# Tap windows kept as a ring of padded rows, in a fused channel-attention and involution kernel

## The chip, the cores and the metric

The kernel runs on one core of a Trainium2 chip. The metric is the device time in microseconds (us) of one launch, the median of the timed runs; the profile is one more execution of the same program. Engines are named as in the profile: PE is TensorE, DVE is VectorE, ACT is ScalarE, POOL is GpSimd, SP is SyncE, which issues most of the transfers.

## What is computed

The input is x of shape (4, 512, 64, 64), float32. Layer 0 is attention over the 4096 pixels of each image; layer 1 is an involution block: a 7x7 stencil whose weights differ from pixel to pixel and are shared by groups of 16 channels.

```python
# layer 0, n = 64*64 pixels
q, k, v = wq@x + bq, wk@x + bk, wv@x + bv          # 128 channels each
attn = softmax(q^T k)                              # 4096 x 4096
x = wo @ (v attn^T) + bo + x
# layer 1, 8 groups of 16 channels, K = 7
o = relu(s1 * (W1 @ x) + b1)                       # 128 channels
w = Ws @ relu(sr * (Wr @ o) + br) + bs             # 49 taps * 8 groups per pixel
y[c, h, w] = sum over taps (i, j): w[g(c), i, j, h, w] * pad(o)[c, h + i, w + j]
out = s3 * (W3 @ y) + b3 + x
```

## The kernel before

`fast_path` does everything; `general_path` is a fallback that a final test on the softmax sums (rls, verdict) selects, and it does not run on these inputs. The outer loop goes over the 4 images (batches, b).

**Attention.** `keys_values(b)` makes k and v for 8 chunks of 512 pixels (tiles xa). `attention(b)` then takes 8 blocks of 512 query pixels (tiles xb; in the last batch the last block is two halves of 256). For each block it goes over 32 key tiles of 128: a score matmul (pss, 128x512), an exponential on ACT (pt, five buffers), a value matmul accumulated in po, and a running sum of pt on DVE (pacc, line 522). TensorE is fed with this steady stream, and everything else is slipped in between: after each step the kernel calls `chores()`.

**Three queues of chores.** They are Python generators; each `yield` ends a step, and the order in which the steps are called is the order of the instructions on each engine.
- `finishing` (`finish_block`): normalises a block of attention (pl, rl), projects it (pwo, line 418, and the addition to xb on line 420), computes o (p, line 428), transposes it (pp) and writes it as pixel rows into a padded image in DRAM (pix, lines 454 to 460), and computes the reduced features (red).
- `taps` (`involution`): the stencil, in units of 4 image rows, 16 units (u) per batch. A unit lives as 128 partitions (two image rows of 64 pixels) x NT = 2 row pairs x 128 channels. The weights of all 49 taps come from a pair of matmuls into PSUM (pw, two banks, one buffer, line 218). Each product is one DVE instruction (line 264) over two taps, that is 2 row pairs x 2 taps x 128 channels = 512 elements per partition (the 49th tap gives one of 256); GpSimd adds it to acc (line 285). One more GpSimd addition (line 294) folds the two halves of acc.
- `closing` (`turn_unit`, `close_chunk`): transposes the sum of a unit on TensorE (pa, line 308) and, for every second unit, applies W3 (py, line 324), adds the result to xb on DVE (line 326) and stores the chunk (line 332).

**The windows of pixels.** A product needs, on the partition of each output pixel, the shifted pixels of its row pair. They are loaded from pix by overlapping reads in `pump()`: for each unit two tiles, with 4 and with 3 horizontal shifts (SHIFTS), each of SR = 9 rows; copies of the first kind have two buffers, of the second one. Each is two transfers of 64 partitions. A unit is begun only when all rows of its window are in pix, that is its own 4 rows and 3 of the next unit, or when the image is complete (line 470).

**Pacing.** The kernel keeps its own estimate of engine time while it writes the program: `pe` for TensorE, and `free` for DVE, GpSimd and DMA, from constants on lines 54 to 60. `pace()` lets out at most TAPS_A_US products per us of TensorE time; `involution` holds a product back while its windows are not due to have landed, or while DVE or GpSimd would be more than 3.5 or 7.5 us behind. `turn_unit` issues its transposes 2 us after the sum is due (line 300). [...] When attention of the last batch has been written, `tail` is set: nothing is held back any more, and every second product is summed by TensorE with an identity matmul into PSUM (accp, line 279) rather than by GpSimd, and joined by a DVE addition (line 293).

The x tiles (xa and xb alike) have six buffers. A tile of xb lives until its chunk is stored.

## Time and profile before

| | |
|---|---|
| device time, median of 3 (lowest to highest) | 2767.58 us (2766.44 to 2768.6) |
| span of the profiled execution | 2761.0 us |
| mean granted TensorE clock | 0.987 |
| products on DVE (line 264, prod), count and busy | 1536, 974.0 us |
| sums on GpSimd (line 285), 512 elements, count and busy | 1412, 1798.2 us |
| window transfers (copies from pix), count and size | 128 of 1152 KB, 128 of 864 KB |
| all transfers | 377.78 MB, mean 137 GB/s |

The page of the profile gives totals per engine, then the span in 40 slices of 69 us (each digit is a share in tenths), then groups of instructions with their count, busy time, mean duration and the idle time ahead of them with what ended it. `prod<-copies,pw` means that the instruction writes prod and reads copies and pw. An fp32 matmul is two instructions in the profile, so 6694 of them are some 3350 matmuls of the program. Idle time of an engine that does not set the pace costs nothing.

### The profile page before, as it was taken

The page shows a single profiled execution, that of the slowest core. Times are in us where ns is not written, and L with a number is a line of the kernel's source. Part 1 is how long each engine was busy: PE and PEld are TensorE (multiplying, and loading weights), DVE is VectorE, ACT ScalarE, POOL GpSimd, SP SyncE. Part 2 cuts the span into 40 slices and gives each one's busy share as a digit, 9 for nine tenths or more (in the row PEclk, how much of TensorE's full clock was granted, in tenths as well). Part 3 has the DMA queues.
Part 4 walks back from the last instruction along what each step waited for, and adds up shares of the span by engine and source line. Part 5 has one row for each costly group of instructions (what it writes and reads, how often), then busy time and mean ns, then how long its engine had stood idle before and what let it go on. Part 6 is the DMA issues. An engine that isn't in the chain of part 4 may idle for free.

```text
span 2761.0 us, 24223 instructions
## 1 busy us (share of the span) xinstructions
PE 2679.7 (97%) x6694; PEld 1205.4 (44%) x6694; DVE 1951.8 (71%) x3091; ACT 894.5 (32%) x1514; POOL 1892.8 (69%) x1548
## 2 busy tenths in 40 slices
PE   8999999999899999999999999999989999999986
PEld 4444444444344444444444444444434444444742
DVE  0356888786586678777566687788747758787886
ACT  2333333332233333333233333333323333333410
POOL 0004887788785478778876477787877548787875
PEclk9999999999999999999999999999999999999998
DMA  6033566668844567766863367766894445666695
GB/s 238 16 64 71 115 144 146 144 136 219 176 113 95 108 145 154 154 141 139 207 158 81 84 114 151 154 136 147 185 227 120 110 88 119 140 143 130 143 195 124
DMA packets 223057, 377.78 MB, mean 137 GB/s; under 512 B 7928, under 2 KB 100288, under 8 KB 222784
## 3 DMA queue, kind: packets, MB, share of 16 engines
q1 hardware_dynamic: 222624, 374.74, 61.6%
q8 instruction: 54, 0.88, 0.1%
q10 hardware_dynamic: 288, 1.42, 0.1%
q14 instruction: 91, 0.75, 0.1%
HBM read 333.29 MB, written 42.77 MB: 136 GB/s over the span
## 4 chain that ended last, share of the span: by engine, by line
PE 91%; DVE 3%; POOL 3%; DMA 1%; issue 0%; ACT 0%; POOLq 0%; SPq 0%; DVEq 0%; ACTq 0%
PE pss L168 32%; PE po L168 32%; PE p L168 4%; PE pq L168 4%; PE py L168 4%; PE pwo L168 4%; PE pk L168 3%; PE pv L168 3%; POOL acc L285 3%; DVE prod L264 2%; PE pw L168 2%; PE pl L168 1%; PE pr L168 1%; PE accp L168 1%; PE pa L308 1%; DMA copies<-pix 1%
## 5 line engine op out<-in xcount | busy, mean ns | idle before, releaser
L285 POOL TENSOR_TENSOR acc<-acc,prod 128x512 f32<-128x512 f32 x1476 | 1844.9, 1250 | 843.8 <-DVE prod L264 538.0
L168 PE MATMUL pss<-q,k 128*128 128x512 f32 (+1 forms) x2112 | 1055.5, 582 | 0.0
L168 PE MATMUL po<-pt,v 128*128 128x512 f32 (+1 forms) x2112 | 1052.4, 580 | 0.0
L264 DVE TENSOR_TENSOR prod<-copies,pw 128x512 f32<-128x512 f32 (+1 forms) x1536 | 974.0, 670 | 89.2 <-POOL acc L285 79.5
L496 ACT ACTIVATE pt<-pss 128x512 f32<-128x512 f32 (+1 forms) x1056 | 616.5, 584 | 1213.7 <-PE pss L168 1080.0
L522 DVE TENSOR_TENSOR pacc<-pacc,pt 128x512 f32<-128x512 f32 (+1 forms) x990 | 672.5, 679 | 451.5 <-ACT pt L496 443.1
L168 PEld LDWEIGHTS po<-pt,v 128*128 128x128 f32 x2112 | 399.6, 190 | 480.8 <-issue 464.4
L168 PEld LDWEIGHTS pss<-q,k 128*128 128x128 f32 x2112 | 393.6, 190 | 466.4 <-issue 455.0
L168 PE MATMUL pwo<-on,wt 128*128 128x512 f32 (+1 forms) x264 | 131.6, 584 | 5.2 <-DVE xb L420 5.2
L168 PE MATMUL py<-accT,wt 128*128 128x512 f32 (+1 forms) x264 | 134.0, 596 | 2.0 <-ACT accT L311 2.0
L168 PE MATMUL pq<-xb,wt 128*128 128x512 f32 (+1 forms) x264 | 120.4, 600 | 8.2 <-DVE xb L326 8.2
L411 DVE RECIPROCAL rl<-pl 128x128 f32<-128x128 f32 x128 | 118.6, 941 | 12.6 <-PE pl L168 12.6
L168 PE MATMUL p<-xb,wt 128*128 128x512 f32 (+1 forms) x264 | 123.3, 593 | 2.4 <-DVE xb L420 2.4
L437 ACT ACTIVATE xb<-xb,vec 128x512 f32<-128x512 f32 (+1 forms) x132 | 93.0, 707 | 98.8 <-PE p L168 94.4
L168 PE MATMUL pk<-xa,wt 128*128 128x512 f32 x256 | 123.4, 623 | 0.3 <-DMA xa<-x_dram 0.3
L168 PE MATMUL pv<-xa,wt 128*128 128x512 f32 x256 | 116.1, 593 | 0.0
L326 DVE SCALAR_TENSOR_TENSOR xb<-py,vec,xb 128x512 f32<-128x512 f32 (+1 forms) x132 | 96.3, 732 | 20.5 <-PE py L168 20.2
L420 DVE SCALAR_TENSOR_TENSOR xb<-pwo,bo,xb 128x512 f32<-128x512 f32 (+1 forms) x132 | 96.2, 732 | 19.7 <-PE pwo L168 19.2
L264 DVE TENSOR_TENSOR acc<-copies,pw 128x512 f32<-128x512 f32 x64 | 43.4, 678 | 89.0 <-PE pw L168 88.9
L520 DVE COPY pacc<-pt 128x512 f32<-128x512 f32 (+1 forms) x33 | 22.3, 677 | 88.5 <-ACT pt L496 88.5
L168 PEld LDWEIGHTS pq<-xb,wt 128*128 128x128 f32 x264 | 51.4, 197 | 68.2 <-issue 54.0
L168 PEld LDWEIGHTS p<-xb,wt 128*128 128x128 f32 x264 | 51.2, 195 | 64.5 <-issue 55.3
(49 smaller groups left out, 875.0 us busy)
## 6 DMA issues: line engine op xcount, KB each, us to landing
copies<-pix SPq DMA_DIRECT2D x128, 1152.0 KB, 13.4
copies<-pix SPq DMA_DIRECT2D x128, 864.0 KB, 14.3
xa<-x_dram SPq DMA_DIRECT2D x32, 1024.0 KB, 11.8
xb<-x_dram SPq DMA_DIRECT2D x32, 1024.0 KB, 6.0
out_dram<-xb SPq DMA_DIRECT2D x31, 1024.0 KB, 9.6
pix<-o1t SPq DMA_DIRECT2D x62, 128.0 KB, 2.5
wt<-wts_dram ACTq DMA_DIRECT2D x1, 1284.0 KB
out_dram<-xb SPq DMA_DIRECT2D x2, 512.0 KB, 3.5
```

The source lines that it names most:

```text
L168: nc.tensor.matmul(o, lhsT=lhsT, rhs=rhs, start=start, stop=stop)
L264: nc.vector.tensor_tensor(prod[:, :, :n, :].rearrange("p t d (g c) -> p t d g c", g=G), image.rearrange("p t d (g c) -> p t d g c", g=G), ...
L285: nc.gpsimd.tensor_tensor(acc[:, :, :n, :], acc[:, :, :n, :], prod[:, :, :n, :], ALU.add)
L308: nc.tensor.transpose(pa[:, t, :], acc[:, t, 0, :], ident)
L326: nc.vector.scalar_tensor_tensor(xt[:, t, :], py, v1(V_S3 + t), xt[:, t, :], ALU.mult, ALU.add)
L411: nc.vector.reciprocal(rl[:, cols], pl[:, cols])
L420: nc.vector.scalar_tensor_tensor(xt[:, t, :], pw, bo[:, t : t + 1], xt[:, t, :], ALU.add, ALU.add)
L437: nc.scalar.activation(xt[:, t, :], xt[:, t, :], AF.Identity, bias=v1(V_B3 + t))
L496: nc.scalar.activation(pt, pss, AF.Exp)
L520: nc.vector.tensor_copy(paccs[k], pt)
L522: nc.vector.tensor_tensor(paccs[k], paccs[k], pt, ALU.add)
```

## The change

The windows are kept in one ring of 12 padded rows with all 7 horizontal shifts (`ring`, 12 x 7 x 128 elements per partition). Each row of an image is loaded into the ring once, instead of once for each of the units whose windows contain it; `low` is the first row still needed and `load` the next to be loaded, and rows go in as their pixels are written and as earlier ones are done with (`pump`). The batches' rows are numbered in steps of 72.

A product now covers 4 or 3 taps that lie above one another (DYS), one horizontal shift at a time, so up to 2 x 4 x 128 = 1024 elements. Where the rows of such a run would cross the end of the ring, it is cut into 2 + 2 or 2 + 1 taps. acc becomes four taps wide and is folded by two GpSimd additions. prods has four buffers of twice the size. `pace` counts taps instead of products. The weights' columns are reordered to match (host side, not shown).

A unit is put into the queue with its own 4 rows; the products with the taps of rows 0 to 3 need no more than these, and those with rows 4 to 6 wait in the generator for the next unit's rows.

In the last batch the last two blocks of attention, instead of the last one, are done in halves of 256 queries, and a step of a half takes two key tiles, so that exponentials and running sums stay 512 wide (the row sums are then added by two matmuls, pl). In the tail the identity matmuls of a unit are joined with its last transposes: the four parts of acc and the two parts of accp, copied to SBUF, are summed by TensorE while they are transposed. Some steps of `finish_block` follow one another faster for the late blocks.

```diff
+WP = W + 2 * PAD
+RING = 12
+STEP = 72
 SR = UR + K - 2
-WP = W + 2 * PAD
-SHIFTS = (0, 4), (4, 3)
-TAPS_A_US = 0.78
+DYS = (0, 4), (4, 3)
+TAPS_A_US = 1.56
 PE_COLUMN = 0.43 / 256
 DVE_OP, POOL_OP = 0.7, 1.28
-COPY_US, X_US, PIX_US, LAND_US = (5.9, 4.4), 3.8, 1.5, 3.0
+DVE_TAPS, POOL_TAPS = (0.16, 0.27), (0.19, 0.55)
+ROW_US, X_US, PIX_US, LAND_US = 2.2, 3.8, 1.5, 3.0
...
-    sapool = pool("sa", 2)
-    sbpool = pool("sb", 1)
     redpool = pool("red", 3)
     work1 = pool("work1", 1)
     work2 = pool("work2", 2)
-    prods = pool("prods", 7)
+    prods = pool("prods", 4)
...
+    ring = const.tile([P, RING, K, P], F32, name="ring")
...
-        due, seen = min(due + TAPS_A_US * (pe - seen), 10), pe
+        due, seen = min(due + TAPS_A_US * (pe - seen), 20), pe
         for _ in range(2):
-            if due < 1 or not step(taps, 1):
+            if due < 2 or not step(taps, 1):
                 break
-            due -= 1
     def pump():
-        for task in list(pending):
-            b, u, part, written = task
-            if not spare[part]:
-                continue
-            pending.remove(task)
-            spare[part] -= 1
-            dx, n = SHIFTS[part]
-            copies = (sapool, sbpool)[part].tile(
-                [P, SR, n, P], F32, tag="s", name=f"copies_{b}_{u}_{part}"
-            )
+        nonlocal load
+        while load // STEP in written:
+            b, row = divmod(load, STEP)
+            rows, us = written[b]
+            end = H + SR - UR if rows == H else rows + PAD - 1
+            n = min(b * STEP + end, low + RING) - load
+            n = min(n, RING - load % RING)
+            if n <= 0:
+                break
             for h in range(2):
-                rows = pix[b % 2][UR * u + h : UR * u + h + SR, dx : dx + W, :]
+                src = pix[b % 2][row + h : row + h + n, :W, :]
                 windows = bass.AP(
-                    tensor=rows.tensor, offset=rows.offset, ap=[[P, W], [WP * P, SR], [1, n * P]]
+                    tensor=src.tensor, offset=src.offset, ap=[[P, W], [WP * P, n], [1, K * P]]
                 )
                 nc.sync.dma_start(
-                    copies[h * W : (h + 1) * W].rearrange("p r x c -> p r (x c)"), windows
-                )
-            free["dma"] = max(free["dma"], written)
-            loaded[b, u, part] = copies, takes("dma", COPY_US[part]) + LAND_US
+                    ring[h * W : (h + 1) * W, load % RING : load % RING + n]
+                    .rearrange("p r x c -> p r (x c)"),
+                    windows,
+                )
+            free["dma"] = max(free["dma"], us)
+            us = takes("dma", ROW_US * n) + LAND_US
+            landing.update((load + i, us) for i in range(n))
+            load += n
+            if row + n == H + SR - UR:
+                load = (b + 1) * STEP
...
-            acc = work2.tile([P, NT, 2, P], F32, tag="acc", name=f"acc_{b}_{u}")
+            acc = work2.tile([P, NT, 4, P], F32, tag="acc", name=f"acc_{b}_{u}")
...
+            accp, ops = None, []
+            base = b * STEP + u * UR
+            for dy0, n in DYS:
+                at = (base + dy0) % RING
+                whole = at + n + NT < RING + 1
+                pieces = [(dy0, n)] if whole else [(dy0, 2), (dy0 + 2, n - 2)]
+                ops += [(x, dy, k) for x in range(K) for dy, k in pieces]
+            for o, (x, dy, n) in enumerate(ops):
+                if o and dy >= DYS[1][0] > ops[o - 1][1]:
+                    low = base + UR
+                    pump()
+                rows = [(base + dy + t * 2) % RING for t in range(NT)]
+                while base + dy + n + NT > load:
+                    yield "wait"
+                landed = max(landing[base + dy + i] for i in range(n + NT))
+                while not tail and (
+                    pe < max(begin, landed)
+                    or free["dve"] > pe + 3.5
+                    or free["pool"] > pe + 7.5
+                ):
+                    yield "wait"
+                free["pool"] = max(free["pool"], takes("dve", DVE_TAPS[0] + DVE_TAPS[1] * n))
+                takes("pool", POOL_TAPS[0] + POOL_TAPS[1] * n)
+                due -= n
+                d0 = dy - DYS[dy >= DYS[1][0]][0]
+                first = x == 0 and dy < DYS[1][0]
+                prod, p0 = acc, d0
+                if not first:
+                    prod, p0 = prods.tile(
+                        [P, NT, 4, P], F32, tag="prod", name=f"prod_{b}_{u}_{o}"
+                    ), 0
+                col = (x * K + dy) * G
+                lines = ring[:, rows[0] : rows[0] + n, x, :]
+                image = bass.AP(
+                    tensor=lines.tensor, offset=lines.offset,
+                    ap=[lines.ap[0], [(rows[1] - rows[0]) * K * P, NT], [K * P, n], [1, P]],
+                )
+                nc.vector.tensor_tensor(
+                    prod[:, :, p0 : p0 + n, :].rearrange("p t d (g c) -> p t d g c", g=G),
+                    image.rearrange("p t d (g c) -> p t d g c", g=G),
+                    pw[:, :, col : col + n * G].unsqueeze(3)
+                    .broadcast_to([P, NT, n * G, GC])
+                    .rearrange("p t (d g) c -> p t d g c", d=n),
+                    ALU.mult,
+                )
+                if first:
+                    pass
+                elif tail and o % 2 and (accp is not None or n > 1):
+                    begin_sum = accp is None
+                    if begin_sum:
+                        accp = ps1.tile(
+                            [P, NT, 2, P], F32, tag=("po", "acc")[u % 2], name=f"accp_{b}_{u}"
                         )
+                    for d in range(0, n, 2):
+                        k = min(2, n - d)
+                        mm(
+                            accp[:, :, :k, :], ident, prod[:, :, d : d + k, :],
+                            begin_sum and d == 0, o + 2 >= len(ops) and d + 2 >= n,
+                        )
+                else:
+                    nc.gpsimd.tensor_tensor(
+                        acc[:, :, d0 : d0 + n, :], acc[:, :, d0 : d0 + n, :], prod[:, :, :n, :],
+                        ALU.add,
                     )
+                yield
+            low = max(low, (b + 1) * STEP if u == NU - 1 else base + UR)
+            pump()
+            if accp is None:
+                for n in (2, 1):
+                    nc.gpsimd.tensor_tensor(
+                        acc[:, :, :n, :], acc[:, :, :n, :], acc[:, :, n : 2 * n, :], ALU.add
+                    )
...
-        for t in range(NT):
-            nc.tensor.transpose(pa[:, t, :], acc[:, t, 0, :], ident)
-        pe_us(0.25)
+        if accp is None:
+            for t in range(NT):
+                nc.tensor.transpose(pa[:, t, :], acc[:, t, 0, :], ident)
+            pe_us(0.25)
+        else:
+            accs = work1.tile([P, CH // P, P], F32, tag="o1t", name=f"accs_{b}_{u}")
+            nc.scalar.copy(accs, accp.rearrange("p t d c -> p (t d) c"))
+            for t in range(NT):
+                parts = [acc[:, t, d, :] for d in range(4)] + [accs[:, 2 * t + d, :] for d in range(2)]
+                for i, part in enumerate(parts):
+                    mm(pa[:, t, :], part, ident, i == 0, i == len(parts) - 1)
...
         rows = top + n // W
-        while begun[b] < NU and (begun[b] * UR + UR + PAD <= rows or rows == H):
-            u = begun[b]
-            begun[b] += 1
-            pending.extend((b, u, part, written) for part in range(2))
-            units.append((b, u))
+        written[b] = rows, us
+        units.extend((b, u) for u in range(top // UR, rows // UR))
         pump()
...
-            blocks[-1:] = [(NCH - 1, off, CH // 2) for off in (0, CH // 2)]
+            blocks[-2:] = [(c, off, CH // 2) for c in (NCH - 2, NCH - 1) for off in (0, CH // 2)]
+        steps = [(k, j) for k, (_, _, n) in enumerate(blocks) for j in range(N // P * n // CH)]
         qs, pts, pos, paccs = {}, {}, {}, {}
         qs[0] = queries(b, *blocks[0])
         def score(m):
-            k, j = divmod(m, nj)
+            k, j = steps[m]
             n = blocks[k][2]
-            pss = ps.tile([P, CH], F32, tag="s", name=f"pss_{b}_{k}_{j}")[:, :n]
-            mm(pss, kt[:, j * P : (j + 1) * P], qs[k])
-            pt = ptpool.tile([P, CH], F32, tag="pt", name=f"pt_{b}_{k}_{j}")[:, :n]
+            pss = ps.tile([P, CH], F32, tag="s", name=f"pss_{b}_{k}_{j}")
+            for i in range(CH // n):
+                key = (j * (CH // n) + i) * P
+                mm(pss[:, i * n : (i + 1) * n], kt[:, key : key + P], qs[k])
+            pt = ptpool.tile([P, CH], F32, tag="pt", name=f"pt_{b}_{k}_{j}")
             nc.scalar.activation(pt, pss, AF.Exp)
             pts[m] = pt
         score(0)
         score(1)
-        for m in range(len(blocks) * nj):
-            k, j = divmod(m, nj)
+        for m, (k, j) in enumerate(steps):
             c, off, n = blocks[k]
+            nj = N // P * n // CH
             if j == 0:
                 pos[k] = ps1.tile([P, CH], F32, tag="po", name=f"po_{b}_{k}")[:, :n]
-                paccs[k] = ps1.tile([P, CH], F32, tag="acc", name=f"pacc_{b}_{k}")[:, :n]
+                paccs[k] = ps1.tile([P, CH], F32, tag="acc", name=f"pacc_{b}_{k}")
...
             pt = pts.pop(m)
-            mm(pos[k], vT[:, j, :], pt, j == 0, j == nj - 1)
-            takes("dve", DVE_OP * n / CH)
+            for i in range(CH // n):
+                key = j * (CH // n) + i
+                mm(
+                    pos[k], vT[:, key, :], pt[:, i * n : (i + 1) * n],
+                    key == 0, key == N // P - 1,
+                )
+            takes("dve", DVE_OP)
             if j == 0:
                 nc.vector.tensor_copy(paccs[k], pt)
             elif j < nj - 1:
                 nc.vector.tensor_tensor(paccs[k], paccs[k], pt, ALU.add)
             else:
-                sums = work1.tile([P, CH], F32, tag="sums", name=f"sums_{b}_{k}")[:, :n]
+                sums = work1.tile([P, CH], F32, tag="sums", name=f"sums_{b}_{k}")
                 nc.vector.tensor_tensor(sums, paccs.pop(k), pt, ALU.add)
```

## The prediction

> **What bounds the kernel now.** I read the page's totals and slices first, then busy time by stage, then the waits inside the odd stages, then single instructions.
>
> ```profile
> PE 2679.7 (97%) x6694; PEld 1205.4 (44%) x6694; DVE 1951.8 (71%) x3091; ACT 894.5 (32%) x1514; POOL 1892.8 (69%) x1548
> PE   8999999999899999999999999999989999999986
> PEclk9999999999999999999999999999999999999998
> DMA  6033566668844567766863367766894445666695
> ```
>
> TensorE is the wall almost everywhere; VectorE and GpSimd have 30% free. The two 8s inside the PE row, near 690 and 2000 us, and its last two digits are where time can be had. How much? The first tap-weight matmul of batches 1 and 2 (the timeline):
>
> ```profile
> 842.50 0.93 PE L168 MATMUL pw<-wt,red 33*128 33x392 f32 x4
> 1508.39 0.93 PE L168 MATMUL pw<-wt,red 33*128 33x392 f32 x4
> ```
>
> One batch takes 665.9 us. Its TensorE work: 8 chunks x 82 matmuls of 512 columns plus 64 for keys and values = 720; consecutive pairs start 1.717 us apart in the timeline, so 0.858 each, 618 us; 16 tap-weight sets at 0.86, 14; 96 transposes at 0.108, 10. Sum 642. So **24 us per batch are lost**, and busy time by stretches of 10 us shows where more than half goes:
>
> ```profile
> 700.00:710.00 10.00, 7.27 (x17) 3.27 (x16) 5.93 (x10) 1.17 (x2) 9.37 (x9) 0.84 1.05 247
> 710.00:720.00 10.00, 3.83 (x12) 1.62 (x11) 5.78 (x9) 0.00 (x0) 9.45 (x9) 0.84 1.05 207
> 720.00:730.00 10.00, 9.27 (x20) 3.75 (x19) 4.13 (x6) 2.16 (x4) 9.37 (x9) 0.81 1.09 255
> ```
>
> Columns: PE, PEld, DVE, ACT, POOL busy, granted clock, DMA share, GB/s. TensorE idles 9.6 us and runs 20.4 us at about 0.83, another 3.4: **13 us**. The same gap stands at 1370 and 2030. GpSimd is full and the DMA engines are saturated. The waits of TensorE from 640 to 760:
>
> ```profile
> PE pa L308 <- POOL acc L294: 6.2, 1, 6.2
> PE pq L168 <- DVE xb L326: 2.7, 1, 2.7
> ```
>
> The transpose of a finished unit waits for GpSimd's backlog, and TensorE, being in order, holds all behind it. In program order that transpose stands ahead of the last key matmuls of the next batch, whose x tile needs one of six slots, some still held by unclosed chunks. The backlog is the cause.
>
> The other loss is the end. The last score and value matmuls start about 2634, the span ends at 2761: **126 us**, in which five units (11 to 15) run one after another, the first product of the first at 2637.5, the last sum at 2744.8, so 21.5 each. The chain of waits there is mostly products, and has this link:
>
> ```profile
> 2681.29 15.06 DMA copies<-pix
> ```
>
> [...]0.66 to 0.84 granted around the gaps and 1.00 away from them, so a removed gap repays more than its length. [...]this trace saturates at about 207 with these windows, and I use the trace.
>
> **The change part by part.** The rows for pricing (groups with shapes apart):
>
> ```profile
> L285 POOL TENSOR_TENSOR acc<-acc,prod 128x512 f32<-128x512 f32 x1412 | 1798.2, 1273 | 838.8 <-DVE prod L264 538.0 <-PE po L168 197.0
> L285 POOL TENSOR_TENSOR acc<-acc,prod 128x256 f32<-128x256 f32 x64 | 46.7, 730 | 5.0
> L264 DVE TENSOR_TENSOR prod<-copies,pw 128x512 f32<-128x512 f32 x1472 | 948.4, 681 | 80.6 <-POOL acc L285 71.2 <-DMA copies<-pix 4.8 <-PE accp L168 1.1
> L264 DVE TENSOR_TENSOR prod<-copies,pw 128x256 f32<-128x256 f32 x64 | 26.6, 416 | 8.7 <-POOL acc L285 8.3
> ```
>
> *Products of 3 or 4 taps.* The two sizes give lines: GpSimd 2.12 ns, VectorE 1.035 ns per element. So 4 taps (1024 elements) cost 2.36 and 1.21 us, 3 taps 1.82 and 0.95. Now a unit is 24 products of 0.681 and one of 0.416 on VectorE, 16.8 us, and 23 sums of 1.273, one of 0.730, one closing of 0.734 on GpSimd, 30.7. Afterwards 14 products where no run of rows crosses the ring's end (one unit in three), 21 where one of the two runs does (2+2 or 2+1 taps). VectorE 15.1, 16.2, 16.2, mean 15.8; GpSimd with two closing sums (1.27+0.73) 28.9, 30.2, 30.0, mean 29.7. **One us less per unit on each.** In mid-batch that is worth nothing: it hides behind TensorE's 1.717 us cadence.
>
> *The ring.* A unit's copies are 2 x (1152+864) KB = 4.13 MB, 20 us at 207 GB/s; four fresh ring rows are 1.84 MB, 8.9 us. Total traffic falls from 378 to about 240 MB, the share from 62% to about 38%. In mid-batch it is hidden anyway; at the end it takes away the 15 us link. The sync queue now waits for a unit's first half to be read, as it now waits for a window's last product; x loads stand behind that. VectorE runs only a few us behind the issue there, so I cost it at nothing.
>
> *Units begun with their own rows.* Today a unit waits for three rows of its neighbour; batch 0's unit 11 starts at 645, and 15 at 801, long after the batch's last rows at 684. Units are 35.5 us apart (538.4, 575.0, 611.9, 644.9) and a chunk takes 73 us, so two units just fit and a backlog stays. With the first taps of the odd unit able to run a chunk earlier, units follow the rows: 12 is done and 13 half done when the last chunk lands, and 2.4 units remain instead of 4. Then x slots are free before the last key chunk asks for one, and the transpose finds its sum ready. I take the **13 us gap as gone at each of three boundaries, 39 us**, and leave the other 11 of each 24 (a 3 us gap near 655, drift). The end of attention moves from 2635 to 2596.
>
> *The last two chunks in halves, two key tiles per step.* Columns on TensorE are the same; 256-column scores already run at 0.43 each. Exponentials and row sums stay 512 wide. The rest is finishing work per half (0.48 for 0.75 us), hidden beside attention. Rows land earlier: relative to the end of attention, about -80, -47, -18 and +14 us (today chunk 6 whole at -46, the halves of 7 at -18 and +14).
>
> *The tail.* Chunk 5 lands at -100. A half unit has 16 us of GpSimd work, a whole one 35 with its gap; rows need 10 us to reach the ring. Unit 9's second half ends at -74, 10 at -39, 11 at -7, so **12 starts at -7 where today 11 starts at +2**. After that VectorE paces: 15.8 of products, 1.5 of closing additions, 2 of waits (today 16.8+0.7+1.5 = 19 became 21.5): 19 each. Units 12 to 15 end at +10, 29, 48, 67. The last close: sum on GpSimd, copy, 12 small identity matmuls, projections: 9, against 8 today (the identity matmuls replace a VectorE addition and a GpSimd one, about even); output and end 10 as now. So +86 instead of +126: **40 us.**
>
> Sum: 2761 - 39 - 40 = 2682 of span; the median lies 6.6 above the profiled span, so 2689.
>
> **The rivals.**
> - *The boundaries keep their gap*: the transpose's due time is an estimate, and a sum 1.3 us late still stops TensorE; more work now lies beside keys and values. For: the gap repeats in all batches. Against: it needs backlog. 2689+39 = 2728.
> - *More is gained*: the 3 us gap near 655 goes too with its clock, 4 each, and units catch up so that half a unit and its waits, 15, less is left: 2689-12-15 = 2662.
> - *Four product buffers choke VectorE.* The plan lets GpSimd lag 7.5 us. Seven buffers of 1.27 cover 8.9; four cover 9.4 with 4 taps, 7.3 with 3, but 5.1 with 2+2 and 4.0 with 2+1. There VectorE, in order, waits 2.4 to 3.5 us at a product; queued behind are the row sums that free the exponentials' five buffers and the residual additions that free two PSUM banks, and TensorE waits for both. If each of the 43 split units costs 2.9 us of TensorE: 2689+125 = **2814, slower.** For: 79.5 us of such waits exist with seven buffers. Against: they sit at the boundaries, and five buffers bridge two steps, 3.4 us.
>
> **How the numbers follow.** The forecast 0.53; gaps kept 0.20; more gained 0.12; choked 0.12; gains that all go elsewhere, within 0.2%, 0.03. The unknown costs: [...]the split gap by 13 each. Range 2650 to 2740: the first three cases with these bounds. Faster 0.85, same 0.03, slower 0.12.
>
> **What would show it.** Sums of 1024 elements near 2.36 us and products near 1.21. DMA share near 38%. No wait of the transpose above 2 us at 660 to 730; batch period about 653. First product of unit 12 before the end of attention. I am wrong if products wait for sums in mid-batch with the clock below 1.00 there, if the batch period stays at 666, or if the tail after the last scores still exceeds 110 us.

## The result, and the profile after

| | before | after |
|---|---|---|
| device time, median (lowest to highest), us | 2767.86 (2766.44 to 2768.6) | 2693.32 (2691.42 to 2695.14) |
| ratio, 95% interval | | 0.9731 [0.9714, 0.9748] |
| span of the profiled execution, us | 2761.0 | 2689.5 |
| periods of the three whole batches, us | 661.5, 665.9, 665.7 | 649.5, 652.0, 652.0 |
| last value matmul of the last batch ends, us | 2635.1 | 2595.6 |
| from there to the end (the tail), us | 125.9 | 93.9 |
| one unit per, in the middle of the last batch, us | 39.8 | 36.7 |

The forecast was 2689 us with a range of 2650 to 2740. Of the 71.5 us of span, 39.6 came in the three whole batches (12.0 + 13.9 + 13.7), nearly all of it at the boundaries between them (from the row-sum matmul of a batch's last block to that of the next batch's first, 161.5 us became 147.2), and 32.0 in the tail. The last row is the mean distance of the tap-weight matmuls from unit 1 to unit 10 of the last batch; it includes the long first step, from unit 1 to unit 2, of which more below.

The page of after, the totals and the slices:

```profile
PE 2653.6 (99%) x6932; PEld 1237.2 (46%) x6932; DVE 1910.1 (71%) x2635; ACT 894.4 (33%) x1495; POOL 1818.1 (68%) x1187
...
PE   8999999999999999999999999999999999999998
...
PEclk9999999999999999999999999999999999999999
DMA  7023223235614233323450423333453242332532
```

The two 8s inside the PE row are 9 now and its last two digits 98 instead of 86, the clock is at 9 (90% or more) in every slice, and the DMA row is thin except at the boundaries.

The timeline of after, TensorE: the first tap-weight matmul of batches 1 and 2, and the end of attention in the last batch.

```profile
830.73 0.93 PE L175 MATMUL pw<-wt,red 33*128 33x392 f32 x4
...
1482.74 0.93 PE L175 MATMUL pw<-wt,red 33*128 33x392 f32 x4
...
2592.83 2.75 PE L175 MATMUL po<-pt,v 128*128 128x256 f32 x12
2595.42 1.03 PE L175 MATMUL pl<-sums,ones 128*128 128x256 f32 x4
2596.38 0.93 PE L175 MATMUL pw<-wt,red 33*128 33x392 f32 x4
```

The two starts are 652.0 us apart, against 665.9 before. The last value matmuls end at 2595.6, and unit 12 starts right behind them, at 2596.38.

After, the stretches of 10 us in which TensorE idled 9.6 us before (columns as in the prediction):

```profile
700.00:710.00 10.00, 10.00 (x27) 4.57 (x26) 0.69 (x1) 2.44 (x5) 3.61 (x2) 1.00 1.05 216
710.00:720.00 10.00, 9.16 (x25) 3.79 (x24) 5.70 (x12) 3.65 (x6) 6.74 (x8) 1.00 1.04 217
720.00:730.00 10.00, 10.00 (x25) 4.50 (x24) 6.36 (x12) 3.58 (x6) 7.50 (x8) 1.00 0.79 282
```

Nearly full, at full clock, while the DMA engines are saturated in the first two (shares of 1.05 and 1.04), as they were. GpSimd has 3.6 to 7.5 us of work in 10 instead of 9.4. All waits of TensorE from 640 to 760, after:

```profile
PE pwo L175 <- DVE xb L463: 2.6, 1, 2.6
PE pss L175 <- ACT q L425: 0.8, 1, 0.8
```

The wait of the transpose for GpSimd is gone. A wait of pwo for an addition to xb is there, of 2.6 us where it was 1.7 before (near 655), of which more below.

The groups of after with shapes apart, sums on GpSimd and the first of the two closing additions:

```profile
L315 POOL TENSOR_TENSOR acc<-acc,prod 128x1024 f32<-128x1024 f32 x255 | 602.0, 2361 | 538.3 <-DVE prod L291 519.1 <-PE pa L175 3.0
L315 POOL TENSOR_TENSOR acc<-acc,prod 128x768 f32<-128x768 f32 x297 | 539.8, 1818 | 78.6 <-DVE prod L291 57.9
L315 POOL TENSOR_TENSOR acc<-acc,prod 128x256 f32<-128x256 f32 x140 | 102.4, 731 | 86.7 <-DVE prod L291 86.0
L324 POOL TENSOR_TENSOR acc<-acc 128x512 f32<-128x512 f32 x60 | 79.9, 1332 | 4.7
```

and products on VectorE:

```profile
L291 DVE TENSOR_TENSOR prod<-ring,pw 128x1024 f32<-128x1024 f32 x264 | 312.7, 1210 | 1.4 <-POOL acc L315 1.4
L291 DVE TENSOR_TENSOR prod<-ring,pw 128x768 f32<-128x768 f32 x308 | 282.2, 944 | 35.2 <-POOL acc L315 29.6 <-DMA ring<-pix 5.6
```

The prices were worked out from two smaller sizes as 2.36, 1.82, 1.21 and 0.95; measured are 2.361, 1.818, 1.210 and 0.944. In all, traffic is 240.07 MB.

### The profile page after: what moved, and what is told of

It is laid out like the page before. It is cut to its first block, busy times and chain, and to the rows that moved or that the text cites. A ratio compares the mean times of both kernels' runs of the same rounds, so it can differ in the third digit from the quotient of the medians.

```text
span 2689.5 us, 23125 instructions
## 1 busy us (share of the span) xinstructions
PE 2653.6 (99%) x6932; PEld 1237.2 (46%) x6932; DVE 1910.1 (71%) x2635; ACT 894.4 (33%) x1495; POOL 1818.1 (68%) x1187
## 2 busy tenths in 40 slices
DMA packets 109285, 240.07 MB, mean 89 GB/s; under 512 B 6296, under 2 KB 24928, under 8 KB 109024
## 3 DMA queue, kind: packets, MB, share of 16 engines
q1 hardware_dynamic: 108864, 237.10, 35.7%
## 4 chain that ended last, share of the span: by engine, by line
PE 96%; POOL 2%; DVE 1%; issue 0%; DMA 0%; ACT 0%; SPq 0%; POOLq 0%; ACTq 0%; DVEq 0%
PE pss L175 33%; PE po L175 33%; PE pq L175 4%; PE p L175 4%; PE pwo L175 4%; PE pv L175 4%; PE py L175 4%; PE pk L175 3%; PE pw L175 2%; POOL acc L315 2%; PE pl L175 1%; PE pr L175 1%; DVE prod L291 1%; PE accp L175 1%; PE pp L491 1%; PE pvt L383 1%
## 5 line engine op out<-in xcount | busy, mean ns | idle before, releaser
L315 POOL TENSOR_TENSOR acc<-acc,prod 128x768 f32<-128x768 f32 (+3 forms) x1059 | 1693.6, 1617 | 847.9 <-DVE prod L291 802.3
L538 ACT ACTIVATE pt<-pss 128x512 f32<-128x512 f32 x1024 | 611.1, 597 | 1220.4 <-PE pss L175 1180.5
L291 DVE TENSOR_TENSOR prod<-ring,pw 128x512 f32<-128x512 f32 (+3 forms) x1092 | 894.2, 848 | 125.5 <-DMA ring<-pix 74.8
L569 DVE TENSOR_TENSOR pacc<-pacc,pt 128x512 f32<-128x512 f32 x956 | 662.1, 693 | 396.0 <-ACT pt L538 392.8
L175 PEld LDWEIGHTS po<-pt,v 128*128 128x128 f32 x2176 | 410.8, 190 | 469.7 <-issue 446.1
L175 PEld LDWEIGHTS pss<-q,k 128*128 128x128 f32 x2176 | 404.9, 190 | 460.8 <-issue 441.5
L324 POOL TENSOR_TENSOR acc<-acc 128x512 f32<-128x512 f32 x120 | 123.4, 1028 | 9.4
L479 ACT ACTIVATE xb<-xb,vec 128x512 f32<-128x512 f32 (+1 forms) x136 | 93.8, 694 | 83.1 <-PE p L175 79.0
L463 DVE SCALAR_TENSOR_TENSOR xb<-pwo,bo,xb 128x512 f32<-128x512 f32 (+1 forms) x136 | 96.9, 716 | 22.9 <-PE pwo L175 22.5
L291 DVE TENSOR_TENSOR acc<-ring,pw 128x1024 f32<-128x1024 f32 (+1 forms) x84 | 78.9, 958 | 29.0 <-PE pw L175 28.7
L567 DVE COPY pacc<-pt 128x512 f32<-128x512 f32 x34 | 23.5, 692 | 88.1 <-ACT pt L538 88.0
L175 PEld LDWEIGHTS pwo<-on,wt 128*128 128x128 f32 x272 | 51.9, 192 | 70.0 <-issue 48.6
## 6 DMA issues: line engine op xcount, KB each, us to landing
ring<-pix SPq DMA_DIRECT2D x38, 896.0 KB, 11.9
```

What stands on the lines that cost most here:

```text
L175: nc.tensor.matmul(o, lhsT=lhsT, rhs=rhs, start=start, stop=stop)
L291: nc.vector.tensor_tensor(prod[:, :, p0 : p0 + n, :].rearrange("p t d (g c) -> p t d g c", g=G), image.rearrange("p t d (g c) -> p t d g c ...
L315: nc.gpsimd.tensor_tensor(acc[:, :, d0 : d0 + n, :], acc[:, :, d0 : d0 + n, :], prod[:, :, :n, :], ALU.add,)
L324: nc.gpsimd.tensor_tensor(acc[:, :, :n, :], acc[:, :, :n, :], acc[:, :, n : 2 * n, :], ALU.add)
L463: nc.vector.scalar_tensor_tensor(xt[:, t, :], pw, bo[:, t : t + 1], xt[:, t, :], ALU.add, ALU.add)
L479: nc.scalar.activation(xt[:, t, :], xt[:, t, :], AF.Identity, bias=v1(V_B3 + t))
```

## Experiments

All are edits of the kernel after, but for the two that say before. Times are medians; ratios are to the kernel before, run on the same chip beside each.

| run | us | ratio [95%] | batch period | attention ends | tail | one unit per |
|---|---|---|---|---|---|---|
| whole window written before a unit is queued | 2692.1 | 0.9729 [0.9713, 0.9745] | 652.0 | 2598.4 | 94.1 | 36.3 |
| rows read once more | 2690.8 | 0.9721 [0.9705, 0.9738] | 649.9 | 2594.1 | 95.0 | 36.7 |
| first product waits for the whole window | 2735.9 | 0.9890 [0.9874, 0.9907] | 661.5 | 2625.9 | 106.8 | 38.9 |
| the same, five product buffers | 2723.0 | 0.9840 [0.9823, 0.9856] | 658.5 | 2617.8 | 104.0 | 38.9 |
| products of two taps | 2716.2 | 0.9818 [0.9802, 0.9835] | 646.4 | 2579.0 | 132.3 | 41.7 |
| one block halved | 2698.2 | 0.9754 [0.9738, 0.9770] | 652.0 | 2594.8 | 100.8 | 37.8 |
| four blocks halved | 2697.4 | 0.9747 [0.9731, 0.9764] | 652.0 | 2603.3 | 93.8 | 35.5 |
| five product buffers | 2681.4 | 0.9696 [0.9683, 0.9709] | 648.4 | 2586.7 | 92.4 | 36.7 |
| three product buffers | 2715.4 | 0.9820 [0.9806, 0.9833] | 656.4 | 2611.6 | 102.3 | 36.7 |
| join of the tail on VectorE | 2704.9 | 0.9779 [0.9765, 0.9792] | 651.9 | 2597.6 | 103.9 | 36.7 |
| before, seven x tiles, five product buffers | 2731.3 | 0.9871 [0.9855, 0.9888] | 652.0 | 2600.8 | 128.5 | 40.1 |
| before, five product buffers | 2789.3 | 1.0079 [1.0063, 1.0096] | 671.8 | 2659.5 | 128.2 | 40.1 |

(Batch period: first tap-weight matmul of batch 1 to that of batch 2. Attention and tail are from the profiled execution, us.)

### Units begun with their own rows: worth nothing

```diff
+    begun = {b: 0 for b in range(B)}
...
-        units.extend((b, u) for u in range(top // UR, rows // UR))
+        while begun[b] < NU and (begun[b] * UR + UR + PAD <= rows or rows == H):
+            units.append((b, begun[b]))
+            begun[b] += 1
```

> The changed kernel with one part undone: a unit is put into the queue only when all rows of its window (its own four and three of the next unit) are written, as in the kernel before. Theory A (the own-row start is what empties the backlog ahead of the boundaries): fewer units are done when the next batch begins, the transpose of a unit waits for GpSimd again in two or three of the boundaries (10 us and more each) and the tail holds at least one unit more (19 us): 2745 to 2755 us, ratio to the kernel before near 0.995. Theory B (the units already run ahead because a unit no longer waits for free copy buffers, or the order of the last key matmuls was the point): boundaries stay without a gap, batch period 650 to 653, and only the tail grows, by half a unit to one unit: 2700 to 2715 us, ratio 0.976 to 0.981. B is a little likelier to me, since TensorE's instructions keep the changed kernel's order at the boundary.

Measured: 2692.1 us, no different from after (2693.3). Boundaries and tail are as in after, and unit 12 of the last batch starts at 2599.2, 0.8 us after the end of attention, as in after. Theory A, which is the prediction's, falls. Of B, the boundaries came true and the half unit of tail did not.

### Traffic: worth nothing

```diff
+    spill = scratch.tile([60, 2, W, K * P], F32, tag="spill", name="spill")
...
+            for h in range(2):
+                src = pix[b % 2][row + h : row + h + n, :W, :]
...
+                nc.sync.dma_start(
+                    spill[load % 48 : load % 48 + n, h].rearrange("r w x -> w r x"), windows
+                )
```

> The changed kernel with every ring row read once more, by the same windows, into a scratch tile in DRAM that nobody reads: traffic rises from 240 to about 366 MB, near that of the kernel before (378). Theory A (the saved traffic is hidden and only takes a link out of the tail): batch period stays within 1 us of 652, tail longer by 0 to 8 us: 2693 to 2702 us. Theory B (the saturated transfers made the gap between batches, since the keys' x tiles landed late behind them): gaps of TensorE return at 660 to 730, period 660 to 666, total 2715 to 2735 us.

Measured: 2690.8 us with 366.7 MB in all. The queue line of its page:

```profile
q1 hardware_dynamic: 146592, 363.73, 47.8%
```

That is 363.7 MB in place of 237.1, and no time was lost. Theory A holds; the total and the period (649.9) even lie 2 us below after, just outside its ranges. The saved bytes, by themselves, gave no part of the 74 us.

### Starting on rows that are already on chip: 43 us

Here the unit is queued as in the first experiment, and its first product is held until the whole window has landed in the ring:

```diff
-                while base + dy + n + NT > load:
+                first_row, end_row = (dy, dy + n + NT) if o else (0, SR)
+                while base + end_row > load:
                     yield "wait"
-                landed = max(landing[base + dy + i] for i in range(n + NT))
+                landed = max(landing[base + i] for i in range(first_row, end_row))
```

> The changed kernel, with a unit queued only when its whole window is written and its first product held until the whole window has landed in the ring (in the run before, the products of taps of rows 0 to 3 could start with rows that the ring already held). Theory A (what the ring gives is that a unit starts on rows already on chip, and no landing stands between the writing of the last row and the first product): every second unit starts 12 us later, GpSimd idles there, and the units fall behind as in the kernel before; unit 12's transpose stands ahead of the last key matmuls again. Gap of TensorE at 700 to 730 again, period 657 to 666, tail later by 10 to 12 us: 2715 to 2745 us. Theory B (the shorter GpSimd work of larger products carries the gain): 2693 to 2705 us, period 650 to 653.

Measured: 2735.9 us, 43.8 more than the run that differs from it only by this hold. Theory A, with its numbers (period 661.5, tail 12.7 longer). To see the mechanism, follow one chunk: chunk 2 is written to pix, and unit 3, which needs three of its rows, makes its first product. In the timeline of before:

```profile
320.79 1.25 SPq L456 DMA_DIRECT2D pix<-o1t  x2
...
340.87 0.69 DVE L264 TENSOR_TENSOR acc<-copies,pw 128x512 f32<-128x512 f32 x1 [0.40 <-PE pw L168]
```

of after:

```profile
322.26 1.27 SPq L498 DMA_DIRECT2D pix<-o1t  x2
...
326.81 1.22 DVE L291 TENSOR_TENSOR acc<-ring,pw 128x1024 f32<-128x1024 f32 x1 [0.40 <-PE pw L175]
```

and of the kernel with the hold:

```profile
319.08 1.26 SPq L500 DMA_DIRECT2D pix<-o1t  x2
...
347.83 1.22 DVE L293 TENSOR_TENSOR acc<-ring,pw 128x1024 f32<-128x1024 f32 x1 [0.48 <-PE pw L176]
```

The first line of each is the write of the pixels on the sync queue, the second the first product of unit 3 on VectorE. From one to the other it takes 20.1 us before, 4.6 after, and 28.8 with the hold. In after the unit begins with the taps of rows 0 to 3, which lie in the ring already and do not depend on that write; the first products that need the three new rows come at 344.8. With the hold, lateness is handed on: unit 2 itself makes its first product at 310.8 (291.6 in after, 301.8 before) and is not done when the rows of unit 3 land. The hold is also somewhat harder than what before did, since in a ring of 12 rows a window can be completed only when the unit ahead is through its first half; so its 43.8 us are not exactly the ring's share of the 74. Nor does a run separate, for the kernel before, the time of the loads from the wait for a free copy buffer.

Why does this show at the boundary? A block of attention lasts 73 us and brings two units, so the rows come at one unit per 36.5 us, and a unit that is late can hardly catch up. The tap-weight matmuls of batch 1 show where the lateness arises. Unit 2 starts 44.7 us after unit 1 in after, 50.9 before and 60.4 with the hold; from unit 2 to unit 10 the units are 35.9, 39.0 and 37.2 us apart. So with the hold most of the lateness arises at one unit and is then carried along, while before it also grew from unit to unit. (The last column of the table is a mean over all these and does not tell the two apart.) Counted from the first unit of the batch, unit 12 starts 28 us later than in after with the hold and 39 before. This is what stands in front of GpSimd when the batch ends. Waits of TensorE from 640 to 760 with the hold:

```profile
PE pss L176 <- ACT pt L542: 6.6, 1, 6.6
PE pa L343 <- POOL acc L326: 2.1, 1, 2.1
PE pwo L176 <- DVE xb L465: 1.6, 1, 1.6
```

The longest is not the transpose this time. The timeline of ScalarE, then of VectorE, with the hold:

```profile
734.13 0.60 ACT L542 ACTIVATE pt<-pss 128x512 f32<-128x512 f32 x1 [9.58 <-DVE pacc L571]
...
718.51 0.42 DVE L293 TENSOR_TENSOR prod<-ring,pw 128x256 f32<-128x256 f32 x1 [1.75 <-POOL acc L317]
720.94 0.69 DVE L293 TENSOR_TENSOR prod<-ring,pw 128x512 f32<-128x512 f32 x1 [2.01 <-POOL acc L317]
723.37 0.42 DVE L293 TENSOR_TENSOR prod<-ring,pw 128x256 f32<-128x256 f32 x1 [1.74 <-POOL acc L317]
...
732.33 1.10 DVE L293 TENSOR_TENSOR prod<-ring,pw 128x512 f32<-128x512 f32 x2 [0.80 <-POOL acc L317]
733.35 0.69 DVE L571 COPY pacc<-pt 128x512 f32<-128x512 f32 x1
```

From 711 to 733 VectorE waits 0.8 to 2.6 us for a buffer at nearly every product, because GpSimd has not yet taken up the one before. The copy that starts the running sum (pacc, L571) is queued behind these products and runs at 733.35, right after the last of them; the exponentials run out of their five buffers (ScalarE idles 9.58 us), and TensorE waits 6.6 us for a score bank.

Is the returned gap then only a shortage of buffers? One more buffer, with the hold kept:

```diff
-    prods = pool("prods", 4)
+    prods = pool("prods", 5)
```

> The kernel in which a unit waits for its whole window in the ring (2735.9 us, batch period 661.6), with five product buffers instead of four. There the transpose of unit 12 stands ahead of the last key matmuls again, but the trace puts the longest wait of TensorE (6.6 us near 730) on VectorE's products, each waiting 0.8 to 2.0 us for a buffer that GpSimd holds, with the row sum queued behind. Theory A (late units fill GpSimd at the boundary, and a buffer more only shifts the wait): period 655 to 660, total 2715 to 2728 us. Theory B (the returned gap is the shortage of buffers): period 647 to 651, total 2690 to 2705 us.

Measured: 2723.0 us, period 658.5. The buffer gives 12.9 us, about as much as without the hold (below); 42 us of the hold remain (2723.0 against 2681.4), and from 640 to 760 TensorE still waits 4.2 us for a score bank and 2.3 for the transpose. Theory A.

### The gap of before: late units, and an order that leaves no way round them

In before the last key matmuls stand behind the transpose of unit 12 in TensorE's order, because their x tile finds no slot. The timeline of before:

```profile
719.26 0.69 PE L308 MATMUL pa<-ident,acc 128*128 128x128 f32 x2 [6.17 <-POOL acc L294]
719.74 5.64 PE L168 MATMUL pk<-xa,wt 128*128 128x512 f32 x8
```

That x tile was issued at 693.8 and landed 15.7 us later, near 709.5; so it was on chip while TensorE waited the 6.17 us for the sum, and the key matmuls came only behind the transpose.

Seven x tiles change that; they need the room of two product buffers, so a control has these alone.

```diff
-    xpool = pool("x", 6)
+    xpool = pool("x", 7)
...
-    prods = pool("prods", 7)
+    prods = pool("prods", 5)
```

> The kernel before with seven x tiles instead of six; to make room product buffers go from seven to five. Theory A (the gap between batches comes from the x slots: with none free, the last key matmuls stand behind the transpose of unit 12 in TensorE's order, and that transpose waits for GpSimd): the gap at 700 to 730 is gone, period about 653 instead of 666, tail unchanged at 126 us: 2725 to 2735 us, ratio 0.986. Theory B (the backlog of GpSimd itself makes the gap, wherever the last key matmuls stand): no gain or a few us lost, 2765 to 2780 us.

> The kernel before with five product buffers instead of seven and nothing else, the control for the run with seven x tiles. Theory A (product buffers don't bind in mid-batch): 2766 to 2772 us, gap at 700 to 730 as in the kernel before. Theory B (VectorE choked by fewer buffers, as the rival of the prediction has it): 5 to 60 us slower, products waiting for sums outside the boundaries.

Measured: 2731.3 and 2789.3 us. The seventh x tile alone is worth 58 us on top of the control. Waits of TensorE from 640 to 760, with seven:

```profile
PE pq L168 <- DVE xb L326: 1.0, 1, 1.0
```

And the three longest with six:

```profile
PE pq L168 <- DVE xb L326: 5.4, 1, 5.4
PE pwo L168 <- DVE xb L420: 3.7, 1, 3.7
PE pa L308 <- POOL acc L294: 2.7, 1, 2.7
```

In the timeline with seven, the last matmuls of keys and values now come ahead of the transpose of unit 12:

```profile
710.38 3.60 PE L168 MATMUL pv<-xa,wt 128*128 128x512 f32 x8
...
728.78 0.38 PE L308 MATMUL pa<-ident,acc 128*128 128x128 f32 x2
```

The units are as late with seven x tiles as before (one per 40.1 us, unit 12 of batch 0 at 685.9 against 684.3), the tail is no shorter, and yet the gap is gone. For the run with seven theory A holds. So a backlog does not make a gap by itself; it does where an instruction that waits for it stands ahead of work that need not. For the control theory A falls and B holds: with five buffers of two taps the period grows by 5.9 us, and the two longest waits are for additions on VectorE. The seventh tile took most of these too (5.4 to 1.0 and 3.7 to 0.4), so the 58 us are not the transpose's alone; how they divide is not shown.

### Products of two taps: 23 us more, in the tail

```diff
-    prods = pool("prods", 4)
+    prods = pool("prods", 8)
...
-                pieces = [(dy0, n)] if whole else [(dy0, 2), (dy0 + 2, n - 2)]
+                pieces = [(dy0, 2), (dy0 + 2, n - 2)]
...
-                        [P, NT, 4, P], F32, tag="prod", name=f"prod_{b}_{u}_{o}"
+                        [P, NT, 2, P], F32, tag="prod", name=f"prod_{b}_{u}_{o}"
```

> The changed kernel with products of at most two taps (2+2 and 2+1 in every run of rows), eight product buffers of half the size, so that the bytes of buffers stay. VectorE and GpSimd each gain about 1 us of work per unit. Theory A (sizes are worth the 1 us a unit only): units run some us later, TensorE's order at the boundary stays, period 652 to 655, tail 4 to 8 us longer: 2697 to 2712 us. Theory B (the larger products are what keeps the backlog away): gap back at the boundaries, period 660 to 666, 2730 to 2750 us.

Measured: 2716.2 us, which neither theory had. The period fell, to 646.4, with no wait of TensorE from 640 to 760 at all (of the 5.6 us, 3.6 are those of a buffer shortage in after, below); the tail grew to 132.3. Attention ends 16.6 us earlier than in after, and the tail is 38.4 longer. Its timeline: the last value matmuls, then the second tap-weight matmul of unit 11 and those of unit 12.

```profile
2577.12 1.89 PE L175 MATMUL po<-pt,v 128*128 128x256 f32 x8
...
2594.32 0.92 PE L175 MATMUL pw<-wt,red 33*128 33x392 f32 x2
...
2611.12 0.93 PE L175 MATMUL pw<-wt,red 33*128 33x392 f32 x4
```

Attention is over at 2579.0 and unit 11 is still to come; in after it was unit 12. By counts and mean durations a unit takes 31.4 us of GpSimd's time here (29.7 in after, 30.7 before) and 17.1 of VectorE's (15.7 and 16.8). So the run undoes more than the change brought, since it has 28 products per unit where before had 25, and more than the 1 us that was expected of it. But the units came every 41.7 us, 5 more than in after, and GpSimd's 1.7 us do not account for that. What holds them is not shown. At most two products are let out per step, which is 4 taps here and up to 8 in after, so a unit that has fallen behind catches up more slowly; this is argued only. The run shows once more that late units need not cost TensorE anything, as long as they stand in no one's way: they cost in the tail.

### Product buffers: the fourth is needed, and a fifth pays

The 2.6 us wait of after is the prediction's choke, once a batch. In the timeline of after, VectorE and then TensorE:

```profile
1310.80 0.95 DVE L291 TENSOR_TENSOR prod<-ring,pw 128x768 f32<-128x768 f32 x1 [1.11 <-POOL acc L315]
1313.23 0.96 DVE L291 TENSOR_TENSOR prod<-ring,pw 128x768 f32<-128x768 f32 x1 [1.48 <-POOL acc L315]
1315.66 0.95 DVE L291 TENSOR_TENSOR prod<-ring,pw 128x768 f32<-128x768 f32 x1 [1.47 <-POOL acc L315]
1316.53 0.75 DVE L463 SCALAR_TENSOR_TENSOR xb<-pwo,bo,xb 128x512 f32<-128x512 f32 x1
...
1317.33 1.41 PE L175 MATMUL pwo<-on,wt 128*128 128x512 f32 x2 [2.62 <-DVE xb L463]
```

Three products wait 1.1 to 1.5 us each for a buffer; the addition to xb (L463) behind them frees a bank that pwo needs. Stretches of 10 us of after:

```profile
1310.00:1320.00 10.00, 7.38 (x18) 3.36 (x18) 5.16 (x7) 1.29 (x3) 9.63 (x5) 0.90 0.33 105
1320.00:1330.00 10.00, 10.00 (x23) 4.42 (x22) 5.67 (x7) 0.80 (x2) 9.58 (x6) 0.93 0.33 105
```

Adding the fifth buffer is the one-line edit shown above, alone.

> The changed kernel with five product buffers instead of four. In the changed kernel TensorE still waits 2.6 us once per batch (at 1315, pwo waits for a residual addition of VectorE) with the clock at 0.90 to 0.93 around it; VectorE's products there wait 1.1 to 1.5 us each for a buffer that GpSimd holds, and the addition is queued behind them. The kernel with products of two taps and eight half-size buffers has no such wait and a period of 646.5 instead of 652. Theory A (four buffers do choke VectorE, once a batch): the wait goes, period 646 to 649, total 2675 to 2685 us. Theory B (GpSimd's backlog, not the number of buffers, sets it): 2690 to 2695 us.

Measured: 2681.4 us, period 648.4: 11.9 us less than after, and the fastest of all kernels run here. The same stretches with five:

```profile
1310.00:1320.00 10.00, 9.79 (x27) 4.37 (x26) 5.95 (x8) 1.86 (x3) 9.69 (x5) 1.00 0.24 89
1320.00:1330.00 10.00, 9.78 (x27) 4.34 (x26) 3.03 (x4) 3.05 (x5) 9.53 (x7) 1.00 0.33 107
```

TensorE is back at 9.8 of 10 and at full clock. Theory A. And with three (`prods = pool("prods", 3)`):

> The changed kernel with three product buffers instead of four. Theory A (the rival of the prediction is right on the mechanism, and four buffers are only just enough): three cover 7.1 us of GpSimd with 4 taps, 5.5 with 3 and 3.0 to 3.8 with the split ones, against a planned lag of 7.5, so VectorE waits at many products in mid-batch, the clock falls there and the total rises by 30 us or more, 2725 to 2800 us. Theory B (buffers don't matter to TensorE): 2692 to 2700 us.

Measured: 2715.4 us, period 656.4. Theory A has the mechanism but not the size: the loss is 22 us, not 30 and more. The waits of TensorE in the whole run show where:

```profile
PE pwo L175 <- DVE xb L463: 18.4, 8, 5.8
```

VectorE's products wait 255 times for a sum in this run, 142.6 us in all (in after 74 times, 50.5 us), but TensorE waits for an addition to xb only eight times, 18.4 us in all: a product that waits cost TensorE here only what was queued behind it.

### The join of the tail: 10 to 12 us

```diff
-            if accp is None:
-                for n in (2, 1):
-                    nc.gpsimd.tensor_tensor(
...
+            for n in (2, 1):
+                nc.gpsimd.tensor_tensor(
...
+                if n == 2 and accp is not None:
+                    nc.vector.tensor_tensor(acc[:, :, :2, :], accp, acc[:, :, :2, :], ALU.add)
...
+        for t in range(NT):
+            nc.tensor.transpose(pa[:, t, :], acc[:, t, 0, :], ident)
```

> The changed kernel with the join of the tail undone: sums of TensorE (accp) are added to acc by VectorE and acc is folded by two GpSimd additions, and a transpose follows, instead of the copy and 12 small matmuls. Per tail unit VectorE gains an addition of 0.68 us and GpSimd two of 1.33 and 0.73. Theory A (about even, as the prediction has it; VectorE paces the tail): 4 x 0.7 us more and 1 to 3 us at the last close: 2694 to 2700 us. Theory B (GpSimd's additions stand in the path of each unit): 4 x 2 us and more, 2701 to 2708 us.

Measured: 2704.9 us, 11.6 more. Of the 12.0 us of span, 10.0 are in the tail, where alone the edit acts; why attention ends 2.0 later is not shown. Theory B. The waits of a unit's transposes for GpSimd's folding, in the whole run, which in after come to 1.8 us:

```profile
PE pa L341 <- POOL acc L323: 9.5, 4, 3.6
```

In the tail of after TensorE is busy for 77.3 us of the 94.0 from 2596 to 2690; the first join takes it 2.8 us there (24 instructions, 2621.3 to 2624.1), and the four joins add up to 14.2 us of busy time. That TensorE has room for these, while additions on GpSimd stand between one unit and the next, is the author's reading of the two runs. The undoing is not the tail of before: with acc four taps wide the folding takes two GpSimd additions, where before took one.

### Halves: one block less, and two more

```diff
-            blocks[-2:] = [(c, off, CH // 2) for c in (NCH - 2, NCH - 1) for off in (0, CH // 2)]
+            blocks[-1:] = [(NCH - 1, off, CH // 2) for off in (0, CH // 2)]
```

> The changed kernel with only the last block of attention in halves, as in the kernel before, instead of the last two. Theory A (units 8 to 12 run back to back on GpSimd, so the earlier rows of block 6 aren't waited for): 2692 to 2697 us. Theory B (rows set the start of the tail): unit 12 starts 10 us later or more, 2703 to 2712 us.

Measured: 2698.2 us. Unit 12 starts at 2606.8, 10.4 later than in after, as theory B has it, but the total is 4.8 more, between the theories.

```diff
+            blocks[-4:] = [(c, off, CH // 2) for c in range(NCH - 4, NCH) for off in (0, CH // 2)]
```

> The changed kernel with the last four blocks of attention in halves instead of the last two. In the changed kernel unit 7 of the last batch waits for the rows of block 4 (written at 2424.6, landed near 2437) and units 8 to 12 then follow each other at some 33 us. Theory A (that wait sets when the tail begins): the first half of block 4 comes some 36 us earlier, units 8 to 12 move forward by up to 10 us, tail shorter by 4 to 10 us: 2684 to 2690 us. Theory B (GpSimd's queue sets it, the rows don't): 2692 to 2697 us.

Measured: 2697.4 us, a miss. Unit 8 does start 13.3 us earlier (2452.2), so the wait for block 4's rows was real. But the halves lengthen attention by 7.7 us (TensorE runs 7252 instructions instead of 6932), and the quick steps of `finish_block` are for the last two chunks only, so the second half of block 5 is written at 2533.3, where the whole of it was written at 2497.2. Unit 12 again starts at the end of attention. Both differences to after are small beside the intervals of the ratios, which overlap.

## Why the prediction was right, and where it was not

- **TensorE is the wall, and the gaps between batches go.** Right, to a microsecond: 39 forecast, 39.6 measured; end of attention 2596 forecast, 2595.6 measured; period about 653 forecast, 652.0 measured. With the step that was to bring it about wrong (below), such closeness is in part luck.
- **"The backlog is the cause."** Half of it. The runs with seven x tiles and with two-tap products have as late units as before and no such gap. It takes late units and, in the order of one engine, something that waits for them ahead of work that need not: in before the transpose ahead of the last key matmuls (TensorE waits 6.2 us), with the hold mostly VectorE's products ahead of the row sum (TensorE waits 6.6 us).
- **What took the backlog away: "With the first taps of the odd unit able to run a chunk earlier, units follow the rows."** The units do follow the rows, but the queue rule to which the prediction gave this is worth nothing (2692.1 without it). The ring does it, by keeping the rows that units share on chip, so that no load stands between the last row and the first product; undone, that costs 43.8 us. The prediction costed the ring as traffic, found it hidden, and was right on that (126 MB more: no loss); it counted the ring's latency at the end only (the 15 us link) and not in mid-batch. The sync queue's waits, which it costed at nothing, are there: VectorE's products wait 74.8 us for ring rows in all of after, where they waited 4.8 for copies before, and the period is the forecast one all the same.
- **Products of three or four taps: "worth nothing" in mid-batch.** Right for TensorE, whose period is even 5.6 us shorter without them. The microsecond per unit was right as work (GpSimd 30.7 before and 29.7 after, VectorE 16.8 and 15.7), but not as pace: with two taps, in 28 products rather than the 25 of before, the units come 5 us further apart, and the run is 22.9 us longer.
- **The tail: 40 forecast, 32.0 measured.** The term that was mis-sized most is the start: the first product of unit 12 was to come 7 us before the end of attention, which was named as a sign, and comes 2.6 after it (its tap-weight matmul 0.8 after). The first products of units 12 to 15 stand at 2598.2, 2621.7, 2640.0 and 2659.5, and the last sum ends at 2676.0, so the four units take 77.8 for 74 forecast. From there to the end it is 13.5 for 19 forecast, which made up for more than half of the lost start. What keeps unit 12 from starting earlier is not shown. **"The identity matmuls ... about even"** is not borne out: doing without them, with acc as wide as it is now, costs 11.6. The comparison that the prediction made, with the narrower acc of before and its single addition, was not run.
- **The small gap near 655 stays.** It did, as a wait of pwo. The prediction had it as a remainder, and in after the cause is its third rival: four product buffers choke VectorE, but once a batch, for 2.6 us. (Before, with seven, the late addition was queued behind four products in a row, 651.6 to 654.0, none of which waited.) A fifth buffer is worth 11.9 us. The rival's size (125 us, at every split unit) falls: only 50.5 us of waits for a sum stand on VectorE in all of after, no longer than 2.0 each. Its count was off too: 40 units are split, not 43, since 24 of the 64 have no run that crosses the ring's end.
- **The rest of the margin.** The median lay 6.6 us above the span before and lies 3.8 above it after, which took 2.8 us of the 8 that the tail had missed. That is luck: it depends on which execution was profiled.

## What to carry to other kernels

When a producer and a stencil share a pace, compare the time of one unit with the time in which its rows come (here 36.5 us). Where the two are this close, a lateness is not made up, whether it arises at one unit or at each; it stays invisible in mid-batch and comes out where something waits for the last unit. What the ring gave here was its latency, not its bytes. So keep rows that the next unit shares on chip, order its work so that it begins with these, and ask on which engine a waiting instruction stands ahead of work that need not wait (here the transpose, 6.2 us of TensorE in before). Where buffers between two engines are cut, try one more before going on: here one line gave another 12 us.

## What the runs showed of the hardware

- In after, GpSimd's additions of products to acc and VectorE's products, both fp32, go on in straight lines to 1024 elements per partition: 0.731, 1.275, 1.818 and 2.361 us on GpSimd for 256, 512, 768 and 1024, and 0.410, 0.680, 0.944 and 1.210 on VectorE.
- In after, the same wait of TensorE of 2.6 us stands once in each of three batches, and the granted clock beside it is not the same each time. In batch 1 its stretch of 10 us (1310 to 1320) has a granted clock of 0.90 and the next one 0.93; in batch 2 (1960 to 1980) they have 1.00 and 0.83; in batch 0 (660 to 680) both have 1.00. So in two of three cases a clock below 1.00 stands beside the wait. With the fifth buffer the wait is gone (in the whole run TensorE waits 0.6 us for that addition, in after 7.9), and both stretches of batch 1 have 1.00; the period from batch 1 to batch 2 is 3.6 us shorter (648.4 for 652.0), and batch 1 begins 1.6 us earlier (829.1 for 830.7). In before the granted clock in the boundary gaps spreads wider than the prediction's 0.66 to 0.84: 0.84, 0.84 and 0.81 from 700 to 730, 0.66 and 0.66 from 1370 to 1390, and 1.00, 0.91 and 0.75 from 2030 to 2060.
- Half as much traffic again on the sync queue (363.7 MB for 237.1) made neither the run nor its period longer (2690.8 us for 2693.3, 649.9 for 652.0). Its share of the DMA engines rose only from 35.7% to 47.8%.
